# Scans with block loads on ScalarE's queue, later statistics and split stores at the turns

## The chip, the cores and the metric

The kernel runs on one core of a Trainium2 chip. The metric is the device time of one execution in microseconds (us), the median of the runs shown. Five engines of the core appear below: TensorE (PE, with its weight loads as PEld), VectorE (DVE), ScalarE (ACT), GpSimd (POOL) and SyncE (SP). DMAs are issued by SP, by ScalarE and by GpSimd; each of these engines issues in the order of its own instructions, and a DMA that has to wait holds what stands behind it on that engine.

## The reference

The input `x` has the shape (4, 48, 256, 256), float32. Four layers follow one another, each as `x = x + layer(groupnorm(x))`. Layers 0 and 3 are convolution blocks with an 8 by 8 FFT filter; the change doesn't touch them. Layers 1 and 2 are chains of scans, and they are the concern here:

```python
def step(w, b):
    def f(carry, inp):
        nxt = inp + _conv1d(carry, w, b)   # 5 taps, 48 to 48 channels, along the line
        return (nxt, nxt)
    return f
# down: over the rows h = 0 .. 255        up: back over the rows, same weights
# right: over the columns w = 0 .. 255    left: back over the columns
```

Every step needs the line before it, so a scan is a chain of 255 small convolutions. The layer's output is the result of the left scan added to `x`. The group norm of the next layer needs mean and variance of that sum, so they are gathered in the left scan.

## The kernel before

**Pairs.** The four images are two pairs (`NP` = 2), each with 2 x 48 = 96 partitions. The partition's halves hold, by the stage, two images or two interleaved halves of a line. The two pairs are independent chains, and the kernel alternates between them line by line, so that TensorE works for one while VectorE finishes the line of the other.

**A line.** `conv` (L488) issues three matmuls into a PSUM tile `acc`; VectorE then adds bias and the incoming line, which gives the next `line` (L547 down, L587 up, L630 right, L668 left). TensorE's next convolution of that pair needs it. The order of TensorE and VectorE is the order of the program text; SP, ScalarE and GpSimd are ordered by a scheduler.

**Strips and blocks.** A scan goes in strips of `RB` = 8 lines, so 32 strips. The lines of a strip lie in one of three rotating line buffers per pair. What a strip takes in is loaded into the pool `in1` (three buffers per pair) by SP: L525 (down, from `x`), L575 (up), L616 (right, from `up`), L651 (left, from `rt`). Four strips, `BK` = 32 lines, make a block. The tile `blk` of a block comes from the pool `blk1`, which has three buffers, shared by the two pairs.

**Up scan.** At the end of a strip ScalarE copies the lines, turned, into `blk` (L592, two copies per pair). At the end of a block GpSimd stores `blk` to the DRAM tensor `up` (L601). For the last block (`h0 == 0`) each store is cut in two: the part that the first strips of the right scan read (`lo`, 8 columns) and the rest (`hi`).

**Right scan.** It reads strips of `up`. The first two strips load the blocks that were stored earlier first, and the last block apart (L616). Its lines go to the DRAM tensor `rt` (L636).

**Left scan.** At the start of a block SP loads the block's part of `x` into `blk` (L656, two DMAs of 1536 KB per pair). After each strip GpSimd adds the lines onto `blk` (L676, two additions per pair: even and odd lines, `f` = 0 and 1; in the last strip VectorE does it). At the end of a block GpSimd stores `blk` to the next `x` (L690, two DMAs of 1536 KB per pair; the last block in sixteen parts). The statistics of a strip, eight `bn_stats` of 0.68 us (L681), are put on a list, `todo`, and VectorE takes one from it after each row of lines of the next strip:

```python
                    if todo:
                        todo.pop(0)()
```

**The next scan.** After layer 1's left scan the down scan of layer 2 loads strips of the new `x` (L525, two DMAs per pair and strip). After layer 2's left scan layer 3 starts with its weights (L722) and its own strips (L787).

Of the kernel before, what the change touches and what calls it, by code (L numbers as in the profile page):

```python
# [11 lines left out]
ALU = mybir.AluOpType  # L12
# [6 lines left out]
BK = 32  # L19
PW = 16  # L20
BH = BK // 2
RB = 8
# [6 lines left out]
class Net:  # L29
# [466 lines left out]
    def scan_layer(self, n, x, xout, scs, stats):  # L496
        nc, W, H, HB, WB, NP = self.nc, self.W, self.H, self.HB, self.WB, self.NP
        pairs, M, RH = range(NP), W // 2, RB // 2
        with self.tc.manual_schedule(engines={mybir.EngineType.PE, mybir.EngineType.DVE}):
# [19 lines left out]
            for h0 in range(0, H, RB):  # L519
                xin, (ln, _, _) = [], next_lines()  # L520
                for p in pairs:

                    t = own(self.pin, p, [CC, 2, 2, WB, RH, BH], "in")
                    for f in range(2):
                        nc.sync.dma_start(  # L525
                            half(t, f).rearrange("p i e v h w -> p (i e v) (h w)"),
                            x[p, :, :, :, :, f, h0 // 2 : h0 // 2 + RH, :].rearrange(
                                "c i e v h w -> c (i e v) (h w)"
                            ),
                        )  # L530
# [31 lines left out]
            for h0 in range(H - RB, -1, -RB):  # L562
# [26 lines left out]
                for p in pairs:  # L589
                    k = h0 % BK  # L590
                    for e in range(2):
                        nc.scalar.copy(  # L592
                            blk[p][:, :, e, :, k // 2 : k // 2 + RH],
                            inner(ln[p][:, e::2]).rearrange("p h i w -> p i w h"),
                        )
                if h0 % BK == 0:

                    for lo, hi in ((0, RB), (RB, M)) if h0 == 0 else ((0, M),):
                        for p in pairs:
                            for f in range(2):  # L600
                                nc.gpsimd.dma_start(  # L601
                                    self.up[p, :, :, :, h0 // BK, f, lo:hi].rearrange("c i e w h -> c (i e) (w h)"),
                                    half(blk[p], f)[:, :, :, lo:hi].rearrange("p i e w h -> p (i e) (w h)"),
                                )
# [37 lines left out]
            todo = []  # L642
            coming("down", "right")
            for w0 in range(W - RB, -1, -RB):
                (ln, last, _), new = next_lines(), []
                for p in pairs:
# [6 lines left out]
                    if (w0 + RB) % BK == 0:  # L653
                        blk[p] = own(self.pblk, 0, [CC, 2, 2, M, BH], "blk")
                        for e in range(2):
                            nc.sync.dma_start(  # L656
                                half(blk[p], e).rearrange("p i f h w -> p i (f h w)"),
                                x[p, :, :, e, w0 // BK].rearrange("c i f h w -> c i (f h w)"),
                            )
                for r in range(RB - 1, -1, -1):  # L660
# [9 lines left out]
                    if todo:  # L670
                        todo.pop(0)()
                for p in pairs:
                    k = w0 % BK
                    for f in range(2):
                        part = blk[p][:, :, f, :, k // 2 : k // 2 + RH]
                        (nc.vector if w0 == 0 else nc.gpsimd).tensor_tensor(  # L676
# [18 lines left out]
            for f in todo:  # L695
                f()
# [434 lines left out]
```

## Time and profile before

| | |
|---|---|
| median of three runs | 14960.64 us (14956.08 to 14967.43) |
| the profiled execution | 14980.35 us, its span 14978.6 us |
| granted TensorE clock, mean | 0.977 |
| TensorE matmul busy | 13946.2 us (93%) |
| VectorE busy | 4877.0 us (33%) |
| ScalarE busy | 3020.6 us (20%) |
| GpSimd busy | 1441.9 us (10%) |

By the start times of their lines the scans of layer 1 run from 3544 (down), 4209 (up), 4904 (right) and 5567 (left) to 6479 us, those of layer 2 from 6521 to 9454 us. Everything before and after is layers 0 and 3.

A row of the groups of instructions reads: line, engine, operation, output<-input, shapes, count | busy time in us, mean ns of one | idle time of the engine just before them, and what ended most of it. A row of the table of waits reads: who waited <- for whom: us in total, times, the longest. A row of the timeline reads: start, length, engine, line, operation, tiles, count, and in brackets the idle time before it with what ended it. Times of a profile are those of one execution.

### The profile page before, as it was taken

What the parts mean: (1) busy time and instruction counts of PE and PEld (TensorE: products, weight loads), DVE (VectorE), ACT (ScalarE), POOL (GpSimd) and SP (SyncE); (2) the same over time, 40 slices, a digit from 0 to 9 for tenths busy, and PEclk for the clock granted to TensorE, in tenths of its full rate; (3) what the DMA queues carried; (4) which work ended last, traced back from release to release, by engine and by line L of the source; (5) the groups of instructions that cost most, each with busy time, mean ns of one, the idle gap of its engine ahead of it and who ended that gap; (6) DMA issues with size and microseconds to landing.
All of it is one profiled execution on the core that took longest, in us unless ns stands there. A gap on an engine that the chain in (4) does not pass through costs nothing.

```text
span 14978.6 us, 417023 instructions
## 1 busy us (share of the span) xinstructions
PE 13946.2 (93%) x194676; PEld 8914.0 (60%) x194676; DVE 4877.0 (33%) x11205; ACT 3020.6 (20%) x2908; POOL 1441.9 (10%) x1249
## 2 busy tenths in 40 slices
PE   2999999998999997789999977799999999999999
PEld 1444444446777675567777755465656666666666
DVE  5333333333333334433333344222222222222222
ACT  1222222222223000012330000122222222222222
POOL 0000000000000014310000144100000000000000
PEclk9999999999999998899999988899999999999999
DMA  7122222215755877677557767211111110111110
GB/s 160 47 53 47 49 51 49 51 42 102 152 140 142 162 154 158 152 146 153 136 152 156 153 154 164 48 24 19 24 19 20 23 22 17 24 20 23 19 24 18
DMA packets 1165501, 1224.06 MB, mean 82 GB/s; under 512 B 1024900, under 2 KB 1026428, under 8 KB 1102908
## 3 DMA queue, kind: packets, MB, share of 16 engines
q1 hardware_dynamic: 1075388, 750.26, 26.3%
q0 software_dynamic: 88384, 447.12, 10.9%
q8 instruction: 1527, 25.02, 0.7%
q14 instruction: 202, 1.65, 0.0%
HBM read 699.82 MB, written 497.42 MB: 80 GB/s over the span
## 4 chain that ended last, share of the span: by engine, by line
PE 83%; issue 6%; DMA 5%; POOL 4%; DVE 2%; SPq 1%; ACT 0%; DVEq 0%; POOLq 0%; ACTq 0%
PE acc L493 27%; PE pd L882 19%; PE pd L270 13%; PE pp L865 8%; PE pz L834 4%; PE ph L245 3%; DMA blk<-x 3%; POOL blk L676 3%; PE po L910 2%; PE pf L823 2%; PE po L355 2%; PE pf L333 1%; PE py L302 1%; DMA gx<-in_x 1%; PE pt L809 1%
## 5 line engine op out<-in xcount | busy, mean ns | idle before, releaser
L493 PE MATMUL acc<-line,w_down 96*96 96x256 f32 x12240 | 2650.2, 379 | 42.8 <-ACT line L534 24.9
L493 PEld LDWEIGHTS acc<-line,w_down 96*96 96x96 f32 x12240 | 1995.8, 163 | 696.6 <-issue 42.9
L493 PE MATMUL acc<-line,w_left 96*96 96x256 f32 x6120 | 1371.2, 386 | 452.4 <-DVE line L668 452.2
L270 PE MATMUL pd<-main,diag 32*32 32x512 f32 x36864 | 1671.2, 599 | 32.4 <-issue 32.3
L882 PE MATMUL pd<-z_a,diag 32*32 32x512 f32 x37152 | 1673.8, 597 | 5.8 <-DVE g_m L897 5.3
L882 PE MATMUL pd<-z_b,diag 32*32 32x512 f32 x37152 | 1651.7, 596 | 14.4 <-DVE g_a L897 13.4
L493 PEld LDWEIGHTS acc<-line,w_left 96*96 96x96 f32 x6120 | 1013.0, 166 | 810.3 <-DVE line L668 476.4
L493 PE MATMUL acc<-line,w_right 96*96 96x256 f32 x6120 | 1330.0, 380 | 65.5 <-DVE line L627 40.1
L865 PEld LDWEIGHTS pp<-c_idft,z 128*128 128x128 f32 x10240 | 1156.9, 181 | 288.7 <-issue 187.0
L865 PE MATMUL pp<-c_idft,z 128*128 128x128 f32 x10240 | 1224.1, 278 | 19.3 <-ACT z_b L869 18.7
L493 PEld LDWEIGHTS acc<-line,w_right 96*96 96x96 f32 x6120 | 1000.2, 164 | 395.3 <-DVE line L627 42.1
L836 DVE TENSOR_TENSOR z<-pz,mask 128x512 f32<-128x512 f32 x1024 | 701.4, 685 | 1431.2 <-PE pz L834 1431.2
L270 PEld LDWEIGHTS pd<-main,diag 32*32 32x32 f32 x36864 | 594.1, 103 | 656.2 <-issue 534.7
L270 PE MATMUL pd<-rest,diag 32*32 32x512 f32 x18432 | 938.1, 597 | 24.6 <-issue 24.6
L882 PEld LDWEIGHTS pd<-z_a,diag 32*32 32x32 f32 x37152 | 638.5, 103 | 491.6 <-issue 306.0
L882 PEld LDWEIGHTS pd<-z_b,diag 32*32 32x32 f32 x37152 | 593.2, 103 | 490.5 <-issue 304.3
L676 POOL TENSOR_TENSOR blk<-blk,line 96x1024 f32<-96x1024 f32 x248 | 703.9, 2865 | 1075.8 <-DVE line L668 575.2
L630 DVE SCALAR_TENSOR_TENSOR line<-acc,b_right,in 96x256 f32<-96x256 f32 x1020 | 489.4, 480 | 836.2 <-PE acc L493 836.2
L587 DVE SCALAR_TENSOR_TENSOR line<-acc,b_down,in 96x256 f32<-96x256 f32 x992 | 476.0, 480 | 808.6 <-PE acc L493 808.6
L547 DVE TENSOR_TENSOR line<-acc,in 96x256 f32<-96x256 f32 x1020 | 429.3, 421 | 928.0 <-PE acc L493 928.0
L102 ACT ACTIVATE nrm<-nrm 96x2 f32<-96x2 f32 (+1 forms) x4 | 0.8, 204 | 3512.2 <-DVE nrm L101 3512.2
L592 ACT COPY blk<-line 96x1024 f32<-96x1024 f32 x256 | 481.3, 1943 | 934.7 <-DVE line L587 741.4
(138 smaller groups left out, 12063.2 us busy)
## 6 DMA issues: line engine op xcount, KB each, us to landing
in<-x SPq DMA_DIRECT2D x256, 384.0 KB, 10.6
blk<-x SPq DMA_DIRECT2D x64, 1536.0 KB, 28.4
dn<-line POOLq DMA_DIRECT2D x124, 768.0 KB, 9.5
rt<-line POOLq DMA_DIRECT2D x124, 768.0 KB, 10.2
in<-rt SPq DMA_DIRECT2D x124, 768.0 KB, 7.4
in<-dn SPq DMA_DIRECT2D x120, 768.0 KB, 8.0
in<-up SPq DMA_DIRECT2D x240, 384.0 KB, 11.1
up<-blk POOLq DMA_DIRECT2D x56, 1536.0 KB, 23.9
```

Of the source, the lines that this page charges most:

```text
L245: nc.tensor.matmul(ph[to, b, 0 : r1 - r0, :], wi[s, at : at + m], xn[s, r0:r1, :], start=True, stop=True)
L270: nc.tensor.matmul(pd[32 * j : 32 * j + 32, i], diag[s, img // 2, t, :], z[s, R2 * j + t // 3 : R2 * j + t // 3 + R2, t % 3 : t % 3 + W], ...
L493: self.nc.tensor.matmul(acc, w[:, t, :], carry[:, :, t : t + m], start=(t == 0), stop=(t == 2))
L547: nc.vector.tensor_tensor(blocks(inner(line)), blocks(acc), xin[p][:, :, r % 2, :, r // 2, :], ALU.add)
L587: nc.vector.scalar_tensor_tensor(inner(line), acc, bd, new[p][r], ALU.add, ALU.add)
L592: nc.scalar.copy(blk[p][:, :, e, :, k // 2 : k // 2 + RH], inner(ln[p][:, e::2]).rearrange("p h i w -> p i w h"),)
L630: nc.vector.scalar_tensor_tensor(blocks(inner(line)), blocks(acc), br, new, ALU.add, ALU.add)
L676: (nc.vector if w0 == 0 else nc.gpsimd).tensor_tensor(part, part, inner(ln[p][:, f::2]).rearrange("p w i h -> p i h w"), ALU.add)
L834: nc.tensor.matmul(pz[:, b, 0 : 2 * HD], xf[s, q, :], wi[s, :], start=True, stop=True)
L836: nc.vector.tensor_tensor(z[:, q, 0 : 2 * n].rearrange("p (b c) -> p b c", b=2), pz[:, :, 0:n], mask[:, :, 0:n].to_broadcast([128, 2, n]), ...
L865: nc.tensor.matmul(pp[0:n, q // 4, :, q % 4 * PW : (q % 4 + 1) * PW], z[:, q0 + q, k * NM : k * NM + n], self.idft, start=True, stop=True,)
L882: nc.tensor.matmul(pd[32 * j : 32 * j + 32, i, 0:n, :], diag[s, 2 if g == "m" else half, t, :], zt[g][s, R2 * j + t // 3 : R2 * j + t // 3 ...
```

## The change

Four edits, all in `scan_layer`:

1. *Down scan, first strip.* The load of the strip is cut: per half `f`, `i` and `e` one DMA for the blocks 1 to 7 and then one for block 0, 16 DMAs per pair instead of 2. Other strips are loaded as before.
2. *Up scan.* ScalarE's copies into `blk` and the stores of `blk` are in one loop over the parts. In the last strip every copy is cut into `lo` and `hi`, and the `lo` parts are stored by ScalarE's queue; all else is stored by GpSimd.
3. *Left scan, loads and statistics.* The loads of `blk` are issued on ScalarE's queue. The eight statistics of a strip are taken one after each line (of either pair) in the last four rows of the next strip, not one after each row from its first.
4. *Left scan, additions and stores.* They are in one loop by parts and pairs, so that a pair's stores follow its additions. In the last strip VectorE's additions are cut into `lo` and `hi`, `lo` of both pairs first, and ScalarE's queue stores the `lo` parts.

```diff
                     for f in range(2):
-                        nc.sync.dma_start(
-                            half(t, f).rearrange("p i e v h w -> p (i e v) (h w)"),
-                            x[p, :, :, :, :, f, h0 // 2 : h0 // 2 + RH, :].rearrange(
-                                "c i e v h w -> c (i e v) (h w)"
-                            ),
-                        )
+                        rows = x[p, :, :, :, :, f, h0 // 2 : h0 // 2 + RH, :]
+                        if h0:
+                            nc.sync.dma_start(
+                                half(t, f).rearrange("p i e v h w -> p (i e v) (h w)"),
+                                rows.rearrange("c i e v h w -> c (i e v) (h w)"),
+                            )
+                            continue
+
+                        for lo, hi in ((1, WB), (0, 1)):
+                            for i in range(2):
+                                for e in range(2):
+                                    nc.sync.dma_start(
+                                        half(t, f)[:, i, e, lo:hi].rearrange("p v h w -> p v (h w)"),
+                                        rows[:, i, e, lo:hi].rearrange("c v h w -> c v (h w)"),
+                                    )
...
-                for p in pairs:
-                    k = h0 % BK
-                    for e in range(2):
-                        nc.scalar.copy(
-                            blk[p][:, :, e, :, k // 2 : k // 2 + RH],
-                            inner(ln[p][:, e::2]).rearrange("p h i w -> p i w h"),
-                        )
-                if h0 % BK == 0:
-
-                    for lo, hi in ((0, RB), (RB, M)) if h0 == 0 else ((0, M),):
-                        for p in pairs:
-                            for f in range(2):
-                                nc.gpsimd.dma_start(
-                                    self.up[p, :, :, :, h0 // BK, f, lo:hi].rearrange("c i e w h -> c (i e) (w h)"),
-                                    half(blk[p], f)[:, :, :, lo:hi].rearrange("p i e w h -> p (i e) (w h)"),
-                                )
+
+                for lo, hi in ((0, RB), (RB, M)) if h0 == 0 else ((0, M),):
+                    for p in pairs:
+                        k = h0 % BK
+                        for e in range(2):
+                            nc.scalar.copy(
+                                blk[p][:, :, e, lo:hi, k // 2 : k // 2 + RH],
+                                inner(ln[p][:, e::2])[..., lo:hi].rearrange("p h i w -> p i w h"),
+                            )
+                        for f in range(2) if h0 % BK == 0 else ():
+                            (nc.scalar if hi < M else nc.gpsimd).dma_start(
+                                self.up[p, :, :, :, h0 // BK, f, lo:hi].rearrange("c i e w h -> c (i e) (w h)"),
+                                half(blk[p], f)[:, :, :, lo:hi].rearrange("p i e w h -> p (i e) (w h)"),
+                            )
...
                         for e in range(2):
-                            nc.sync.dma_start(
+                            nc.scalar.dma_start(
                                 half(blk[p], e).rearrange("p i f h w -> p i (f h w)"),
                                 x[p, :, :, e, w0 // BK].rearrange("c i f h w -> c i (f h w)"),
                             )
+                ripe, fresh = fresh, []
                 for r in range(RB - 1, -1, -1):
                     for p in pairs:
...
-                    if todo:
-                        todo.pop(0)()
+                        if ripe and r < RB // 2:
+                            ripe.pop(0)()
+                k = w0 % BK
+
+                for lo, hi in ((0, RB), (RB, M)) if w0 == 0 else ((0, M),):
+                    for p in pairs:
+                        for f in range(2):
+                            part = blk[p][:, :, f, lo:hi, k // 2 : k // 2 + RH]
+                            (nc.vector if w0 == 0 else nc.gpsimd).tensor_tensor(
+                                part, part, inner(ln[p][:, f::2])[..., lo:hi].rearrange("p w i h -> p i h w"), ALU.add
+                            )
+                        for e in range(2) if k == 0 else ():
+                            for f in ((0, 1), (1, 2)) if w0 == 0 else ((0, 2),):
+                                f = slice(*f)
+                                (nc.scalar if hi < M else nc.gpsimd).dma_start(
+                                    xout[p, :, :, e, w0 // BK, f, lo:hi].rearrange("c i f h w -> c i (f h w)"),
+                                    half(blk[p], e)[:, :, f, lo:hi].rearrange("p i f h w -> p i (f h w)"),
+                                )
                 for p in pairs:
...
+                            to, t = stats[2 * p + i][:, w0 // RB * 2 + f, :], blk[p][:, i, f, :, k // 2 : k // 2 + RH]
+                            fresh.append(lambda to=to, t=t: nc.vector.bn_stats(to, t))
```

The number of bytes moved and the arithmetic are the same.

## The prediction

> **What bounds the kernel now.** I read the slices first: TensorE is busy nearly everywhere except in slices 16 to 18 and 24 to 26, the two left scans. Then the costliest groups, for the same convolution in the right and the left scan:
>
> ```profile
> L493 PE MATMUL acc<-line,w_left 96*96 96x256 f32 x6120 | 1371.2, 386 | 452.4 <-DVE line L668 452.2
> ...
> L493 PE MATMUL acc<-line,w_right 96*96 96x256 f32 x6120 | 1330.0, 380 | 65.5 <-DVE line L627 40.1
> ...
> L676 POOL TENSOR_TENSOR blk<-blk,line 96x1024 f32<-96x1024 f32 x248 | 703.9, 2865 | 1075.8 <-DVE line L668 575.2
> ```
>
> Both scans have 6120 matmuls of nearly one duration, but TensorE idles 452.4 us ahead of those of the left scans and 65.5 us ahead of those of the right. All of it waits for VectorE's line update, L668, so next the table of waits for what holds VectorE:
>
> ```profile
> DVE st L681 <- POOL blk L676: 507.3, 61, 32.4
> POOL blk L676 <- DMA blk<-x: 500.5, 14, 38.0
> ```
>
> VectorE waits 507.3 us at L681, the statistics, for GpSimd's addition; GpSimd waits 14 times, 500.5 us, for the block load. The statistics stand between line updates, so TensorE stops behind them. The timeline shows both waits; I call 5647.48, where the last strip of a block starts its additions, T0.
>
> ```profile
> 5647.48 8.52 POOL L676 TENSOR_TENSOR blk<-blk,line 96x1024 f32<-96x1024 f32 x3 [10.84 <-DVE line L668]
> ...
> 5656.04 0.69 DVE L681 BATCH_NORM_STATS2 st<-blk 96x6 f32<-96x512 f32 x1 [2.16 <-POOL blk L676]
> 5656.30 0.54 POOL L690 DMA_DIRECT2D x<-blk  x1 [0.29 <-POOL blk L676]
> ...
> 5659.66 1.67 POOL L690 DMA_DIRECT2D x<-blk  x3
> ...
> 5676.72 16.97 SPq L656 DMA_DIRECT2D blk<-x  x4
> ...
> 5715.48 5.63 POOL L676 TENSOR_TENSOR blk<-blk,line 96x1024 f32<-96x1024 f32 x2 [37.54 <-DMA blk<-x]
> 5718.33 0.69 DVE L681 BATCH_NORM_STATS2 st<-blk 96x6 f32<-96x512 f32 x1 [31.92 <-POOL blk L676]
> ...
> 5719.46 34.18 PE L493 MATMUL acc<-line,w_left 96*96 96x256 f32 x144 [30.98 <-DVE line L668]
> ```
>
> In every strip the first statistic waits for three additions (8.52 us) and comes 2.16 us late. A strip then repeats every 22.17 us; the right scan needs 20.72 (the chain of waits, from 7943.30 to 8523.48, 28 strips), so 1.45 us is lost. At a block's end the wait is 31.92 us: pair 1's new block reuses the buffer of pair 0's old one (three buffers, four blocks wanted), so its load goes out only when pair 0's second store has landed (5659.66 plus its 16.9 us) and lands at 5715.48, T0+68. After such a stop the clock is low (columns of the windows: length, busy time and instructions of PE, PEld, DVE, ACT, POOL, then granted clock, DMA share, GB/s):
>
> ```profile
> 5720.00:5725.00 5.00, 5.00 (x13) 3.39 (x12) 0.94 (x3) 0.00 (x0) 3.17 (x2) 0.50 0.71 177
> 5725.00:5730.00 5.00, 5.00 (x24) 3.70 (x23) 3.06 (x6) 0.00 (x0) 5.00 (x3) 0.97 0.54 128
> ```
>
> 13 matmuls in 5 us instead of 24: 144 matmuls take 34.18 us against 31.32 before the stop, 2.9 us more. The seven stops of a scan repeat every 118.2 us; 4 strips of 20.72 are 82.9, so **35.3 us is lost per block**, and a left scan takes 912 us, some 250 over 664.
>
> The turns from up to right cost about 35 us each:
>
> ```profile
> 4871.06 1.13 POOL L601 DMA_DIRECT2D up<-blk  x2 [2.11 <-ACT blk L592]
> 4872.88 3.38 POOL L601 DMA_DIRECT2D up<-blk  x6 [0.69 <-ACT blk L592]
> 4873.77 30.18 SPq L616 DMA_DIRECT2D in<-up  x16
> 4893.85 0.29 DVE L627 COPY line<-in 96x256 f32<-96x256 f32 x1 [24.83 <-DMA in<-up]
> ...
> 4903.70 0.29 DVE L627 COPY line<-in 96x256 f32<-96x256 f32 x1 [9.56 <-DMA in<-up]
> ```
>
> The 16 small loads (24 KB, packets of 256 B) need 30 us on SP while four stores of 1440 KB drain; pair 1 is complete only when the stores are.
>
> **What the Trainium skill says.** "DMA: Bandwidth & Descriptors", section "Issuing engines are not separate DMA queues": another issuing engine saves only its sequencer's time; the transfers share the same engines. So moving the block loads gives no bandwidth; the trace agrees, the DMA share being about 1.0 all through T0+10 to T0+68. The same page, "Queues, rings and completion order": each DMA engine takes turns between queue rows, a packet at a time. The turn agrees: from 4880 to 4888, 222 packets of the hardware queue and 279 of the software queue moved, nearly one for one, but 0.05 MB against 1.97. "TensorE: Matmul & The Clock Gate", "What's actually happening": the clock halves after some 3.4 us of idling; the window above shows it.
>
> **The change part by part.**
>
> *Statistics later.* Same 8 per strip, 0.68 us each, now one after each line of the last four rows. The first is due 11.7 us after the strip's start instead of 2.6; the third addition is done some 4.7 us after it. All ordinary waits go: 1.45 us × 3 per block. Cover on VectorE: a line is due every 1.295 us, update and statistic are 0.48 + 0.68 = 1.16; in the slots that hold a statistic now VectorE still idles 0.22 us for TensorE, so I cost them at nothing. Without that cover 0.1 us a slot would be 51 us (512 slots).
>
> *Block loads on ScalarE's queue.* ScalarE computes nothing in a left scan, so a waiting load blocks nothing there, and on SP the loads of `rt` no longer stand behind it (they end no wait now: nothing). The load still waits for pair 0's store. In the changed kernel's order GpSimd does pair 0's f=1, pair 1's f=1, pair 0's f=0, then both stores of pair 0 (T0+8.8 and T0+9.4, before +8.8 and +12.2), pair 1's f=0, and then **the first addition of the next strip before pair 1's stores**: these leave at T0+23.7 instead of +12.7. Pair 0's two stores follow one another in one queue (12.0 us for the first, 8.3 more for the second), so both land at T0+27 to 29. Then 3.15 MB of pair 1's load, nearly all of 3.15 MB of pair 1's stores and about 1.2 MB of `rt` are in flight, 7 MB. Before, 8.6 MB moved from T0+29.2 to T0+68 (with a part of the following block's load, which is now out later): 221 GB/s. 7 MB take 32 us: **landing at T0+60** (55 if stores and load overlap at the 250 to 280 GB/s of the windows with mixed traffic; 65 if they go one after the other).
>
> *What the stop becomes.* Pair 1's first statistic is due at T0 + 2 × 20.72 = T0+41.4 (it was T0+38.9) and needs one addition after the landing: 60 + 2.85 − 41.4 = 21 us, plus 2.9 for the clock: 24 instead of 35.3. The following strip's additions are queued behind and catch up: they end 11.4 us after the late pair, half a strip before their statistics. Per scan 7 × 11.3 + 4 (first block) = 83 us, **two scans 166 us gained** (96 to 236 for landings at T0+65 and T0+55).
>
> *Up to right.* ScalarE's copies are split, but in the changed order narrow and wide slices alternate, and pair 1's narrow store leaves after all four pairs of copies, at 4875.2 instead of about 4873. No gain there. SP has one load of the next strip ahead of pair 1's four, and ScalarE's queue sends pair 1's first block (3.15 MB) as soon as pair 0's wide store lands, about 4888 (wide stores took 11.7 to 19.4 us), into the drain. Block transfers move in packets of some 14 KB (448 for 6.29 MB); with 16 KB that is 12 for each of 16 DMA engines, each about 1 us at a sixteenth of 250 GB/s and one turn that SP's small packets wait: 12 us, and 3 for the extra load. So 15 us later, two turns: **30 us lost**. Bounds: 5 us won in all, if the smaller queue on GpSimd drains earlier, to 50 lost, if the second block's load joins too.
>
> *First strip of the down scans.* 16 loads per pair instead of 2. Layer 1: all issue after the norm at 3532; 32 × 0.5 us puts pair 1's last issue at 3548, its landing near 3553 against 3545.4 now, so it loses 8 (3 to 14). Layer 2: seven eighths are loaded ahead; only 16 of 12 KB remain, behind the small stores that now leave on ScalarE at about 6481. They suffer from the wide stores as at the other turn, 48 packets per DMA engine at 0.57 us: ready about 6513 against 6521: 7 won (0 to 16; the norm, ready at 6502, is the next thing late). Layer 3: its weights wait for the last store; GpSimd issues 8 instead of 16, and no longer waits for queue slots (1.57 us): 5 won (0 to 6). Sum +4.
>
> **Sum:** 166 − 30 + 4 = 140 us. Against the profiled execution (14980.35, of it 1.75 outside the span) this is 14840; the runs shown have a median 20 us lower, 14960.64, so I forecast **14820**.
>
> **Rivals.**
> *A, likeliest (0.60):* as above; its own range, with the bounds added, 14730 to 14910.
> *B, the load lands no earlier (0.15):* two stores and a load finish together as late as before (T0+66.5 on average). Stop 27.5 + 2.9; gain 2 × (7 × 4.9 + 4) = 77, minus 26: 14910. For it: the DMA engines were full already. Against it: the other block's load leaves the interval.
> *C, slower (0.13):* the delayed stores of pair 1 starve the load at the block's end. If the stores drain first (some 4.3 MB with `rt` from T0+28, at 200 GB/s until T0+50) and the load then needs 28 us, the median landing of a block load on the page, it lands at T0+78: stop 39 + 2.9, 6.6 more than before; 2 × (7 × 6.6 − 4) = 84 lost, and 26 at the turns: 15070. It decides from a landing at about T0+70 on. For it: the stores leave 11 us later, right ahead of the load. Against it: the one-for-one turns seen above.
> *D, the stop nearly goes (0.12):* pair 0's stores, alone in their queue, land at T0+22 and the load at T0+48: stop 9 + 2.9; gain 2 × (7 × 23.4 + 4) − 26 = 310: 14650. Against it: the first store alone took 12 us.
>
> **How the numbers follow.** 0.2% is 30 us, about what a measurement of this kernel can tell from no change. A is faster in nearly all of its range, B mostly, D wholly: 0.81. Same 0.07, from the edges of A and B. Slower 0.12, C. The range of 14680 to 14930 holds A, B and the near edge of D; it leaves out C and most of D.
>
> **What would show it.** Right: the first statistic of a strip waits for nothing in three strips of four; strips of 20.7 us; seven stops per left scan of 16 to 26 us behind the DMA of `blk`; left scans near 830 us; 40 to 55 us at the up-to-right turns; layer 1's start 8 us later. Wrong: stops over 31 us (C) or under 12 (D); TensorE idle behind the packed statistics in the last four rows; a right scan whose loads are late in its third strip.

## The result and the profile after

The changed kernel takes **14795.3 us** (median of 4 runs, 14786.4 to 14797.92) against 14964.03 us before: a ratio of 0.9886, 95% interval 0.9869 to 0.9903, or 169 us less. The forecast was 14820 us. The profiled execution has a span of 14796.1 us and a mean granted clock of 0.981 (before 0.977).

The costliest groups first: the same convolution in the left and in the right scan, and GpSimd's additions.

```profile
L493 PE MATMUL acc<-line,w_left 96*96 96x256 f32 x6120 | 1359.4, 385 | 252.0 <-DVE line L676 252.0
L493 PE MATMUL acc<-line,w_right 96*96 96x256 f32 x6120 | 1338.9, 381 | 103.4 <-DVE line L637 38.9
...
L686 POOL TENSOR_TENSOR blk<-blk,line 96x1024 f32<-96x1024 f32 x248 | 705.8, 2874 | 864.8 <-DVE line L676 445.8
```

TensorE's idle time in the left scans fell from 452.4 to 252.0 us. In the right scans it rose from 65.5 to 103.4. GpSimd's additions are as many as before and as long (2874 ns against 2865). The table of waits says which waits shrank:

```profile
POOL blk L686 <- DMA blk<-x: 419.0, 14, 32.6
...
DVE st L700 <- POOL blk L686: 275.9, 28, 21.6
```

VectorE's wait at the statistics fell from 507.3 us (61 times) to 275.9 (28 times, two at each of 14 stops): the waits of ordinary strips are gone, those at a block's end are shorter. The timeline at the first block's end (T0 = 5656.41, where GpSimd starts the additions of the block's last strip):

```profile
5651.07 0.68 DVE L700 BATCH_NORM_STATS2 st<-blk 96x6 f32<-96x512 f32 x1
5651.96 0.48 DVE L676 SCALAR_TENSOR_TENSOR line<-acc,b_left,in 96x256 f32<-96x256 f32 x1 [0.21 <-PE acc L493]
...
5656.41 8.52 POOL L686 TENSOR_TENSOR blk<-blk,line 96x1024 f32<-96x1024 f32 x3 [9.37 <-DVE line L676]
...
5665.23 1.09 POOL L692 DMA_DIRECT2D x<-blk  x2 [0.29 <-POOL blk L686]
...
5679.93 1.10 POOL L692 DMA_DIRECT2D x<-blk  x2
...
5682.56 27.60 ACTq L663 DMA_DIRECT2D blk<-x  x4
...
5714.24 16.96 POOL L686 TENSOR_TENSOR blk<-blk,line 96x1024 f32<-96x1024 f32 x6 [30.31 <-DMA blk<-x]
5717.10 0.69 DVE L700 BATCH_NORM_STATS2 st<-blk 96x6 f32<-96x512 f32 x1 [19.33 <-POOL blk L686]
...
5718.23 11.95 PE L493 MATMUL acc<-line,w_left 96*96 96x256 f32 x46 [18.39 <-DVE line L676]
```

The first two rows are an ordinary slot: a statistic, then the line update, which still waits 0.21 us for TensorE, so the statistic is hidden. Then both stores of pair 0 leave at T0+8.8, those of pair 1 at T0+23.5; pair 1's new block is asked for at T0+26.2, GpSimd adds at T0+57.8, and TensorE has stood still for 18.4 us.

The turn from up to right, layer 1:

```profile
4859.40 1.26 ACTq L608 DMA_DIRECT2D up<-blk  x2
...
4862.34 31.45 SPq L623 DMA_DIRECT2D in<-up  x16
...
4888.61 0.29 DVE L634 COPY line<-in 96x256 f32<-96x256 f32 x1 [29.57 <-DMA in<-up]
...
4893.27 0.29 DVE L634 COPY line<-in 96x256 f32<-96x256 f32 x1 [4.36 <-DMA in<-up]
...
4895.52 25.89 ACTq L663 DMA_DIRECT2D blk<-x  x4
...
4947.65 0.48 DVE L637 SCALAR_TENSOR_TENSOR line<-acc,b_right,in 96x256 f32<-96x256 f32 x1 [12.95 <-DMA in<-up]
...
4958.35 0.87 DVE L637 SCALAR_TENSOR_TENSOR line<-acc,b_right,in 96x256 f32<-96x256 f32 x2 [10.23 <-DMA in<-up]
```

The two pairs start at 4888.61 and 4893.27 (in the kernel before at 4893.85 and 4903.70, its up scan ending 10 us later). But ScalarE sends four block loads, 6.3 MB (pair 1's first block and pair 0's second), from 4895.52 on, and the third strip's lines come late: the updates at 4947.65 and 4958.35 end waits of 12.95 and 10.23 us for the load of `in`.

Taken from the start times of VectorE's line updates, first to last line of a scan, layers 1 and 2 (us). A landing is read as the end of GpSimd's wait for the block:

| | before | after |
|---|---|---|
| left scans | 911.1, 909.5 | 805.3, 803.2 |
| right scans | 662.2, 662.4 | 686.0, 686.4 |
| last line of up to first convolved line of right | 35.4, 35.5 | 34.9, 35.0 |
| last line of layer 1's left scan to first line of layer 2 | 42.8 | 38.9 |
| landing of pair 1's block, mean of 14 | T0+66.2 | T0+57.4 |

The profiled spans differ by 182.5 us, 13 more than the medians. That much lies in layer 0, which ends 13.4 us earlier in this execution (scale of the norm, L110, at 3507.5 against 3520.9); two kernels with the same layer 0, told of below, have it at 3509.9 and 3519.3. It is scatter between executions.

### The profile page after: what moved, and what is told of

The parts are those of the page before. It is cut to its first block, busy times and chain, and to the rows that moved or that the text cites. A ratio compares the mean times of both kernels' runs of the same rounds, so it can differ in the third digit from the quotient of the medians.

```text
span 14796.1 us, 417160 instructions
## 1 busy us (share of the span) xinstructions
PE 13940.6 (94%) x194676; PEld 8922.0 (60%) x194676; DVE 4880.6 (33%) x11213; ACT 3022.1 (20%) x2916; POOL 1429.3 (10%) x1225
## 4 chain that ended last, share of the span: by engine, by line
PE 89%; DMA 6%; DVE 1%; SPq 1%; issue 1%; POOL 1%; ACT 0%; ACTq 0%; DVEq 0%; POOLq 0%
PE acc L493 32%; PE pd L889 19%; PE pd L270 13%; PE pp L872 8%; PE pz L841 4%; PE ph L245 3%; DMA blk<-x 3%; PE po L917 2%; PE pf L830 2%; PE po L355 2%; PE pf L333 1%; PE py L302 1%; DMA x<-blk 1%; DMA gx<-in_x 1%; POOL blk L686 1%
## 5 line engine op out<-in xcount | busy, mean ns | idle before, releaser
L889 PE MATMUL pd<-z_b,diag 32*32 32x512 f32 x37152 | 1651.0, 596 | 14.0 <-DVE g_a L904 13.1
L493 PE MATMUL acc<-line,w_left 96*96 96x256 f32 x6120 | 1359.4, 385 | 252.0 <-DVE line L676 252.0
L493 PE MATMUL acc<-line,w_right 96*96 96x256 f32 x6120 | 1338.9, 381 | 103.4 <-DVE line L637 38.9
L686 POOL TENSOR_TENSOR blk<-blk,line 96x1024 f32<-96x1024 f32 x248 | 705.8, 2874 | 864.8 <-DVE line L676 445.8
L603 ACT COPY blk<-line 96x1024 f32<-96x1024 f32 (+2 forms) x264 | 482.0, 1889 | 935.7 <-DVE line L596 755.9
## 6 DMA issues: line engine op xcount, KB each, us to landing
blk<-x ACTq DMA_DIRECT2D x64, 1536.0 KB, 23.3
up<-blk POOLq DMA_DIRECT2D x56, 1536.0 KB, 23.8
```

Source lines behind the costliest of these rows:

```text
L493: self.nc.tensor.matmul(acc, w[:, t, :], carry[:, :, t : t + m], start=(t == 0), stop=(t == 2))
L603: nc.scalar.copy(blk[p][:, :, e, lo:hi, k // 2 : k // 2 + RH], inner(ln[p][:, e::2])[..., lo:hi].rearrange("p h i w -> p i w h"),)
L686: (nc.vector if w0 == 0 else nc.gpsimd).tensor_tensor(part, part, inner(ln[p][:, f::2])[..., lo:hi].rearrange("p w i h -> p i h w"), ALU.add)
L889: nc.tensor.matmul(pd[32 * j : 32 * j + 32, i, 0:n, :], diag[s, 2 if g == "m" else half, t, :], zt[g][s, R2 * j + t // 3 : R2 * j + t // 3 ...
```

## The experiments

Two questions stood after the comparison. Which of the three edits of the left scan moved the landing from T0+66 to T0+57? And what made the second stop of the right scans? My theory was that the order of the stores did the first and ScalarE's queue the second. The lengths of scans are again those of the profiled execution, layers 1 and 2. The kernel before was measured again beside each group of runs: its median was 14971.28 us beside the first four experiments (the three single edits and the one with all block loads back on SP), 14970.72 and 14967.41 beside the later ones. In two of the expectations 893 and 787 stand for a second left scan; they are layer 1's scan counted without its first strip (18 us), so 912 and 805 are the figures to compare with.

### Single edits on the kernel before

*Statistics alone.*

```diff
-                    if todo:
-                        todo.pop(0)()
+                        if ripe and r < RB // 2:
+                            ripe.pop(0)()
```

> The kernel before with one edit: the eight statistics of a strip are taken in the last four rows of the next strip, as in the changed kernel. Loads, stores and turns are those of before. Theory: the edit takes away the 1.45 us of each ordinary strip (two per block remain in the table of before besides the stop, four in the first block) and puts the deadline of pair 1's first statistic from T0+38.9 to T0+41.4. The block load still lands at T0+66 (mean of the 14 stops before: 66.3), so a stop is 66.3 + 2.9 - 41.4 = 28 us and a block repeats every 113 us: 5.4 won per block, 14 blocks and the two first blocks: about 87 us faster than before, near 14877. Rival (the transfers set the period): the strips get shorter, the load lands later by the same amount, and under 30 us are won. Rival (VectorE has no room in the last four rows): TensorE loses 0.1 us or more in 512 slots, and the gain shrinks to 35 us.

Measured: 14876.3 us, ratio 0.9938 (0.9923 to 0.9952). Left scans 863.4 and 867.0 us, 90 less in the sum against 87 expected; landing unchanged at T0+66.1. VectorE's waits for the additions:

```profile
DVE st L682 <- POOL blk L677: 397.5, 28, 29.7
```

28 waits instead of 61: only those at a block's end are left. The price of the statistics and the later deadline was right, and neither rival holds.

*Queue alone.*

```diff
-                            nc.sync.dma_start(
+                            nc.scalar.dma_start(
                                 half(blk[p], e).rearrange("p i f h w -> p i (f h w)"),
```

> The kernel before with one edit: the block loads of the left scans are issued on ScalarE's queue instead of SP's. Theory (the order of the stores, not the queue, makes the load land earlier): landing stays at T0+65 to T0+68, the left scans stay within 10 us of 912 and 893, and the right scans get the second stop of the changed kernel (some 23 us in the third strip), because ScalarE sends the first blocks' loads into the turn: 40 to 50 us slower than before, near 15010. Rival (the queue of its own makes the load land earlier): landing at T0+57 to T0+60, 8 us won in each of 14 blocks, 112 us, less the 47 us at the turns: 14900. Rival (the second stop comes from the changed order of the small stores and loads at the turn, not from the block loads): no second stop here, and no change.

Measured: 14982.85 us, ratio 1.0009 (1.0000 to 1.0017): no gain. It is two effects that cancel. The left scans take 889.5 and 895.0 us, 36 less in the sum (landing T0+63.6, a third of the way, which I had not expected), and the right scans 685.6 and 686.1 us, 47 more, with the same stop in the third strip. So the second stop belongs to the queue: here no store at the turn was changed. The 36 us are the landing, 2.6 us in each of 14 stops.

*Stores pair by pair alone.*

```diff
                 for p in pairs:
...
+                    if k == 0 and w0:
+                        for e in range(2):
+                            nc.gpsimd.dma_start(
+                                xout[p, :, :, e, w0 // BK].rearrange("c i f h w -> c i (f h w)"),
+                                half(blk[p], e).rearrange("p i f h w -> p i (f h w)"),
+                            )
...
```

> The kernel before with one edit: in the left scan a pair's two stores follow that pair's additions, so that pair 0's go out at T0+8.8 and T0+9.4; pair 1's still go out at about T0+12.5, ahead of the next strip's additions. Loads on SP, statistics and turns as before. Theory: pair 0's second store lands 3 us earlier, the load goes out at T0+26 and lands at T0+62 to T0+64 (the stores of pair 1 are not late, so the mixture of transfers is that of before): 3 to 4 us won per block, 14 blocks, 40 to 55 us faster, near 14915. Rival (the order of the stores alone makes the whole difference): landing at T0+57.5, 8.8 us per block, 123 us faster. Rival (it is the queue or the delayed stores of pair 1): landing at T0+66, no change.

Measured: 14866.04 us, ratio 0.9933 (0.9918 to 0.9948). Left scans 861.4 and 860.5 us, 99 less in the sum, twice what my theory gave. The load left no earlier, at T0+29.7, but landed at T0+59.1. The order of the stores matters, then, but not by way of an earlier start of the load. SP's queue at the first block's end (T0 = 5631.24):

```profile
5633.78 1.60 SPq L651 DMA_DIRECT2D in<-rt  x2
5660.95 2.57 SPq L656 DMA_DIRECT2D blk<-x  x2
5663.62 3.64 SPq L651 DMA_DIRECT2D in<-rt  x2
5680.02 0.55 SPq L656 DMA_DIRECT2D blk<-x  x1
```

SP issues in order: the loads of `rt` follow 0.10 us after the end of the block loads that had waited ahead of them (5660.95 + 2.57 = 5663.52). In the kernel before (T0 = 5647.48) two loads of `rt` left at T0+2.5 and T0+3.8, as here, but the next two at T0+24.7 and T0+26.0, and only then, from 5676.72 on, four of `blk`. Here two loads of `rt` (one strip, 1.57 MB) stand behind pair 1's block instead of ahead of it, and only one of pair 0's next two block loads follows within 20 us, not both. SP's order is the scheduler's work, and the edit of the stores had moved it. Whether this reordering makes the earlier landing is not shown by this run; it is taken up below.

### Putting edits together and taking one away

*The changed kernel with all block loads back on SP.* The diff is that of the queue, reversed.

> The changed kernel with one edit undone: all block loads of the left scans are issued on SP again. Theory (the order of the stores makes the load land early, the queue makes the second stop of the right scans): landing stays at T0+57 to T0+60, the left scans stay within 10 us of 805 and 787 us, and the stop of 23.5 us in the third strip of both right scans goes: 45 us faster than the changed kernel, near 14750. Rival (the queue makes the landing early): landing back at T0+66, 8.8 us per block lost, 123 us, and 47 won at the turns: 14870. Rival (loads of the lines standing behind a waiting block load on SP): a strip's lines from rt come late, with stops at other strips than the block's end.

Measured: 14756.68 us, ratio to before 0.9856 (0.9840 to 0.9872), 39 us under the changed kernel (46, if each is set against the kernel before that was measured beside it). Left scans 803.1 and 804.3, landing T0+57.2; right scans 662.5 and 661.5, no second stop. My theory held: beside the other two edits the queue brings nothing in the left scans and costs 47 us at the turns.

*The kernel before with statistics and stores edited, no edit at the turns.*

> The kernel before with two edits: statistics in the last four rows and stores pair by pair. No edit at the turns, loads on SP. With both edits the order on GpSimd has the next strip's first addition ahead of pair 1's stores, as in the changed kernel (with the stores alone it had not). Theory: left scans of 803 us as in the changed kernel with its loads on SP, and everything else as before: the edits at the turns are worth no more than 8 us together, so 14757 to 14770, 205 us faster than before. Rival (the two edits only add up: 90 and 99 us in the left scans): 14780. Rival (the small stores on ScalarE's queue and the split first strips carry more than that): 14775 or above, or below 14745 if they cost.

Measured: 14751.6 us, ratio 0.9853 (0.9839 to 0.9868). Left scans 803.1 and 802.7 us, landing T0+57.3. The two edits are worth 215 us together where they gave 90 and 99 alone: with both, pair 1's stores leave at T0+23.5 instead of T0+13.1, the load leaves at T0+25.8 instead of T0+29.7, and it lands 1.8 us earlier than with the stores alone, 25 us in 14 blocks. The edits at the turns are worth nothing that these medians show (14756.68 with them, 14751.6 without).

*Pair 1's stores early, on ScalarE's queue.*

```diff
-                                (nc.scalar if hi < M else nc.gpsimd).dma_start(
+                                (nc.scalar if hi < M or (p and w0) else nc.gpsimd).dma_start(
```

> The changed kernel with the block loads on SP, and pair 1's stores of all blocks but the last on ScalarE's queue, so that no addition of the next strip stands ahead of them: they leave at T0+12 to T0+13 instead of T0+23.5. Theory (the late stores help pair 0's stores to land early and hardly hurt the load): pair 1's load leaves at T0+29 instead of T0+26 and lands at T0+59 instead of T0+57.2; 2 us more in each of 14 stops, 14785. Rival (the late stores starve the load, as my third case had it): landing at T0+50 or earlier, 7 us less in each stop, 14660. Rival (on a queue of their own the stores of the two pairs share evenly, so pair 0's land with pair 1's at T0+30 and both loads go out together as before): landing at T0+64 to T0+66, 7 to 9 us more in each stop, 14870.

Measured: 14745.88 us, ratio 0.9850 (0.9835 to 0.9864). None of the three cases. The load left at T0+33, 7 us later than with the late stores, and still landed at T0+57.0. So the moment of issue isn't what sets the landing. The late stores of pair 1 do not starve the load, and sending them early wins nothing at the landing.

*The first block's loads on SP, later ones on ScalarE's queue.*

```diff
+                        queue = nc.sync if w0 + RB > W - BK else nc.scalar
                         for e in range(2):
-                            nc.scalar.dma_start(
+                            queue.dma_start(
...
```

> The changed kernel with the first block's loads of each left scan (both pairs) on SP, all later ones on ScalarE's queue. At the turn from up to right ScalarE then sends only pair 0's second block, 3.15 MB, instead of 6.3 MB, while the third strip's loads (1.57 MB in packets of 256 B) are on their way. Theory (the second stop is the third strip waiting for block traffic, so it goes by bytes): 3.15 MB less at some 200 GB/s are 16 us less, the stop in the third strip falls from 23.5 to about 8 us (0 to 12), and the kernel stands 30 us under the changed kernel, at 14765. Rival (what counts is that a block load goes out at all while the small packets wait for their turns): the stop stays at 20 us or more. Rival (it was the first block alone, sent earliest): the stop is gone, 14755.

Measured: 14738.55 us (two runs), ratio 0.9846 (0.9826 to 0.9866). Right scans 662.3 and 661.5 us: the stop is gone altogether. The trace takes the ground from under the comparison of 3.15 with 6.3 MB:

```profile
4895.62 0.54 SPq L664 DMA_DIRECT2D blk<-x  x1
...
5485.28 22.58 ACTq L664 DMA_DIRECT2D blk<-x  x2
```

ScalarE's first block load left at 5485 us, near the end of the right scan, and none of ScalarE's fell into the turn. Why pair 0's second block waited so long I don't know. What follows is only that it is enough to keep the first block off ScalarE's queue. Nor does every block load at the turn make a stop: here SP itself sent 1.57 MB of pair 0's first block at 4895.62, ahead of the third strip's loads, and in the kernel before it sent 3.15 MB at 4907.32, both without one. Whether the stop comes from the amount (6.3 MB) or from the second queue beside SP's was not separated.

### What sets the landing

*Pair 0's later blocks not loaded.*

```diff
-                        for e in range(2):
+                        for f in range(4) if p == 0 and w0 + RB < W else ():
+                            to = blk[p][:, f // 2, f % 2].rearrange("p h w -> p (h w)")
+                            nc.scalar.copy(to, bl[:, 0:1].to_broadcast([CC, M * BH]))
+                        for e in range(2) if p or w0 + RB == W else ():
```

> The kernel before with one thing taken out: from the second block on, pair 0's blocks are not loaded from x; the idle ScalarE fills them from the bias with four copies of 96x2048 instead, so pair 0's part of the sum is left out. Order of stores, queues, statistics and pair 1's loads are those of before. In the kernel before, pair 1's load leaves at T0+29 and shares the DMA engines from T0+45 on with pair 0's following block (3.15 MB). Theory (this competing load, not the moment of issue, makes pair 1's load late; storing pair by pair works because it sends the competitor out later and in halves): pair 1's load still leaves at T0+29 and lands at T0+56 to T0+59 instead of T0+66, the stops are 9 us shorter, 14 of them: about 14840. Rival (the delay comes from stores and from the small loads of lines): landing at T0+64 to T0+66, within 30 us of before.

Measured: 14928.08 us, ratio 0.9970 (0.9959 to 0.9982). Landing T0+63.4: the competing load costs 2.8 us, not 9. My theory fell. Another took its place: pair 1's block lands when the bytes that SP and GpSimd have queued ahead of it and beside it have moved. The DMA view, from T0+5 to the landing (63.5 us), of the kernel before at a block of layer 2 (q1 is SP's queue):

```profile
DMA packets 1165, 13.60 MB, mean 214 GB/s; under 512 B 165, under 2 KB 165, under 8 KB 165
...
q1 hardware_dynamic: 716, 7.29, 59.3%
```

The same stretch (53.6 us) with stores pair by pair:

```profile
DMA packets 983, 11.70 MB, mean 218 GB/s; under 512 B 139, under 2 KB 139, under 8 KB 139
...
q1 hardware_dynamic: 533, 5.37, 52.1%
```

And in the changed kernel (53.1 us), where q10 is ScalarE's queue:

```profile
DMA packets 1122, 12.96 MB, mean 244 GB/s; under 512 B 160, under 2 KB 160, under 8 KB 160
...
q1 hardware_dynamic: 406, 2.80, 20.3%
...
q10 hardware_dynamic: 267, 3.85, 31.5%
```

The software queue (q0, GpSimd's stores) moves 6.29 MB in each. With stores pair by pair 1.9 MB fewer pass ahead of the landing, at nearly the same rate (218 against 214 GB/s): 1.9 MB at 215 GB/s are 8.8 us for a landing that comes 9.9 us earlier at these two blocks. The kernel with pair 1's stores early moved 11.77 MB at 226 GB/s, though its load left 7 us later. At nearly one rate fewer bytes up to a landing and an earlier landing are almost one statement. Which bytes matter can only be seen by taking some out. Pair 0's following load, taken out above, is a first answer: over the 14 stops 12.22 MB moved at 209 GB/s instead of 13.36 at 218, so 1.14 MB less won 2.8 us, about half of what they take at the old rate (1.14 MB at 218 GB/s are 5.2 us). Why the rate fell isn't known.

*The last strip of a block not loaded from `rt`,* the two loads that stood ahead:

```diff
-                        nc.sync.dma_start(t.rearrange("p r i h -> p r (i h)"), self.rt[p, :, w0 : w0 + RB, :])
+                        if w0 % BK == 0:
+                            nc.scalar.copy(t.rearrange("p r i h -> p (r i h)"), bl[:, 0:1].to_broadcast([CC, RB * W]))
+                        else:
+                            nc.sync.dma_start(t.rearrange("p r i h -> p r (i h)"), self.rt[p, :, w0 : w0 + RB, :])
```

> The kernel before, with the last strip of each block of the left scan not loaded from rt: ScalarE fills its tile from the bias (96x2048, about 2 us a copy), so those lines are left out. In the kernel before these two loads, 1.57 MB, go out on SP at about T0+23 to T0+28 just ahead of pair 1's block load. Theory (pair 1's load lands when the bytes ahead of it and beside it have moved, at 210 to 220 GB/s; 13.6 MB are moved from T0+5 to its landing, storing pair by pair puts one strip's lines behind the block load and so lands at T0+59): without these bytes the load lands at T0+59 to T0+60 instead of T0+66.2, every stop is 6.5 us shorter, 14 stops: 90 us faster than before, near 14880. Rival (the moment at which pair 0's stores land is all that counts): landing at T0+64 to T0+66.

*The second strip not loaded,* as many bytes, at another place (`w0 % BK == 2 * RB`):

> The kernel before, with the second strip of each block not loaded from rt but filled by ScalarE in the same way: as many bytes are left out as with the last strip, but they would have moved ahead of T0, when the DMA engines are a third busy. Theory (only the bytes between T0 and the landing count): landing stays at T0+65 to T0+67, and the kernel is within 30 us of before. Rival (the bytes of a whole block set its period): as much is won as with the last strip left out, about 90 us.

Measured: without the last strip 14848.87 us (two runs), ratio 0.9920 (0.9900 to 0.9939), landing T0+57.6, somewhat earlier than expected; without the second 14967.84 us, ratio 1.0001 (0.9992 to 1.0011), landing T0+66.5. The DMA view of one block each, from T0+5 to the landing, first without the last strip, then without the second:

```profile
DMA packets 908, 11.57 MB, mean 222 GB/s; under 512 B 128, under 2 KB 128, under 8 KB 128
...
DMA packets 1159, 13.53 MB, mean 215 GB/s; under 512 B 165, under 2 KB 165, under 8 KB 165
```

The same bytes are worth 118 us in one place and nothing in the other, so what counts is whether they stand between T0 and the landing. Over the 14 stops the run without the last strip moved 1.83 MB less than the kernel before, at the same rate (219 and 218 GB/s): 8.4 us, for a landing that comes 8.6 us earlier. In these two runs, then, bytes ahead of the block load cost their full time, and those of the later load beside it about half.

### A faster version

The stop is the way of one buffer from pair 0's store to pair 1's load. Half a buffer goes round sooner:

```diff
-                        blk[p] = own(self.pblk, 0, [CC, 2, 2, M, BH], "blk")
+                        blk[p] = [own(self.pblk, 0, [CC, 2, M, BH], "blk") for _ in range(2)]
...
+                        for f in range(2):
+                            for e in range(2):
+                                nc.sync.dma_start(
+                                    half(blk[p][f], e).rearrange("p i h w -> p i (h w)"),
+                                    x[p, :, :, e, w0 // BK, f].rearrange("c i h w -> c i (h w)"),
+                                )
```

> The changed kernel with the block loads on SP, and each block in two tiles, one for even and one for odd lines (six buffers of 16 KB per partition instead of three of 32), each loaded, added to, stored and released by itself. Theory (the stop is the way of one buffer from pair 0's store to pair 1's load, so half a buffer goes round faster): pair 0's first half is stored at T0+6 to T0+9, lands at about T0+18, its statistics are taken by T0+17 to T0+20, so 1.57 MB of pair 1 can leave near T0+20 and land at T0+42 to T0+48; the first addition needs no more. Stop 4 to 9 us, and 2 for the clock: 11 to 14 us won in each of 14 blocks, 14580 (14550 to 14620). Rival (the DMA engines are the bound: 18.9 MB per block at 200 GB/s are 94 us, 11 us over four strips): 14630 whatever the buffers do. Rival (packets of 8 KB instead of 16 KB and twice the issues eat it): within 30 us of 14757.

Measured: **14588.4 us**, ratio to before 0.9746 (0.9729 to 0.9762), 207 us under the changed kernel. Left scans 751.3 and 734.6 us. The groups:

```profile
L493 PE MATMUL acc<-line,w_left 96*96 96x256 f32 x6120 | 1382.5, 389 | 106.3 <-DVE line L678 106.3
L493 PE MATMUL acc<-line,w_right 96*96 96x256 f32 x6120 | 1329.3, 379 | 32.6 <-DVE line L635 20.4
```

The timeline at one block's end (T0 = 5716.28), the load of the first half and the two halves of the stop:

```profile
5736.30 9.31 SPq L665 DMA_DIRECT2D blk<-x  x4
...
5756.75 2.86 POOL L688 TENSOR_TENSOR blk<-blk,line 96x1024 f32<-96x1024 f32 x1 [11.48 <-DMA blk<-x]
...
5759.64 0.69 DVE L700 BATCH_NORM_STATS2 st<-blk 96x6 f32<-96x512 f32 x1 [2.00 <-POOL blk L688]
...
5766.74 14.08 POOL L688 TENSOR_TENSOR blk<-blk,line 96x1024 f32<-96x1024 f32 x5 [7.14 <-DMA blk<-x]
5769.60 0.69 DVE L700 BATCH_NORM_STATS2 st<-blk 96x6 f32<-96x512 f32 x1 [7.90 <-POOL blk L688]
```

The first half leaves at T0+20.0 and is added at T0+40.5, the second at T0+50.5; the stop is two waits of 2.00 and 7.90 us. The load leaves just as the last of pair 0's four statistics ends (5736.23), and by the table of waits SP waits 4.4 us for the statistics ahead of a block load in this stretch, so these may be what is late next; that wasn't tried. The turns, too, took 19.0 us instead of 35, which I had not expected: ScalarE waits on its queue (3.41 us for a store, 4.68 with nothing shown), its last wide copies (those for the `hi` parts) come after that, and so six of the eight wide stores leave at 4864.6 to 4868.0 us, when eight of the sixteen small loads have been issued (4852.95 to 4864.23).

*With the wide stores put last,* on SP behind the first strip's loads:

> The kernel with half tiles, and the wide parts of the last block of the up scan stored on SP behind the first strip's loads of the right scan (one of the eight stays ahead of them). With half tiles the turn took 19 us instead of 35, because ScalarE's queue held the wide copies back, so that part of the small loads passed ahead of the wide stores. Theory (small loads are slow only while wide stores are in flight): the first line of the right scan comes 12 to 15 us after the last of the up scan; but the second strip's last parts wait for the wide stores, which now land some 30 us after the turn, so that a stop of 5 to 15 us appears in the second strip, and the sum is within 10 us of 14588. Rival (the wide stores drain faster undisturbed and the second strip comes in time): 10 us less at each turn, 14568. Rival (stores on SP hold up the loads behind them): a stop of over 20 us, 14610 or more.

Measured: 14604.34 us, ratio 0.9759 (0.9742 to 0.9775), slower by 16 us than without it, where I expected at most 10 either way. The right scan starts 12.6 us after the up scan, and a stop in its second strip takes that back, as the theory had it (the two right scans are 13 and 16 us longer): from the last line of up to the end of the right scan 687.8 and 690.8 us, against 680.9 and 681.1 with half tiles alone. That is the whole difference.

## Why the prediction was right, point by point

| step | predicted | measured |
|---|---|---|
| left scans, both | −166 | −212 |
| turns up to right | +30 | +47 |
| layer 1's start | +8 | +3.5 |
| layer 2's start | −7 | −3.9 |
| layer 3's start | −5 | about −2 |
| sum | −140 | −167 |
| medians | −140 (14820) | −169 |

The sum came closer than its terms: the left scans won 46 us more and the turns lost 17 us more than I had reckoned, and that these two errors partly cancel is luck.

**Ordinary strips** went as predicted, and the packed statistics cost nothing: the slot still shows 0.21 us of idle time.

**The stop** was the mis-sized term. Its chain was right: stores at T0+8.8 and +23.5, load issued at about T0+26 (I had T0+27 to 29), deadline T0+41.4. The landing was T0+57.4, not 60, and the low clock after the shorter stop cost 1.8 us, not 2.9 (in the first 5 us after it the granted clock was 0.64, before 0.50): 57.4 + 2.9 − 41.4 + 1.8 = 20.7 us per block instead of 24. That is 3.3 us in 14 blocks, the missing 46 us. I took 7 MB after the stores' landing at 221 GB/s, the rate of the kernel before. The trace has 12.96 MB at 244 GB/s over the whole stretch. Over all 14 stretches of a kernel the mean is 244 in the changed kernel and 245 in the one that differs from it only in the first block's queue. It is 223 with all block loads on SP, and 223 with ScalarE's queue alone. So the queue brings the higher rate, but only beside the other two edits; why is open. I had reckoned with no gain in bandwidth from it.

**What I credited was partly wrong.** I had the queue as harmless in the left scan and the late stores of pair 1 as a risk. The runs show that the late stores decide nothing at the landing, and that the queue takes the place of an effect that I had not seen at all: with the new order of stores SP would have put one strip's lines behind the block load. With ScalarE's queue those lines move beside it (2.80 MB on q1 before the landing), and at the higher rate the load lands at the same time (T0+57.4 against 57.2 on SP).

**The turns** have the right cause in the wrong place. I let ScalarE's block loads collide with pair 1's small loads in the first strip. But they left at 4895.5, not 4888, when both first strips were in; the first stop is 0.5 us shorter than before. They met the third strip's loads instead, which the prediction named as a sign against it, and the second block's load did join, which was its worst case (50 lost): 23.8 and 24.0 us per right scan instead of 15.

**The starts** are within their bounds. Layer 1: first line 24.7 us after the scale of the norm instead of 23.3, and 2.1 us more behind it. Layer 3: from the last line of the left scan to the end 5522.0 us, in eight kernels with the old order 5522.3 to 5525.7.

**The rivals.** B and D are out by their landings (T0+66.5, T0+48). C (T0+78) is out by its landing too, and its cause by the run with pair 1's stores early: T0+57.0 against 57.2. B's stop has a slip: its own figures, 66.5 + 2.85 − 41.4, give 28.0 us, not 27.5, some 6 us in 14 blocks.

## What to carry to other kernels

When DMA engines are full, count the bytes that stand ahead of the transfer that ends the wait, queue by queue, and not the moment of its issue: taking 1.57 MB out of the right place won 118 us, out of another place nothing. The rate has to be measured too: here it was 209 to 245 GB/s, by the mixture. A load that moves to an idle engine's queue also moves in time, since nothing there holds it back (pair 1's first block left at 4895.5 us instead of 5513.1): look where it lands in the stage before. Where two edits come together, run each alone: here one of three, the queue, brought all of the loss at the turns and, beside the other two, none of the gain.

## What the runs showed that I had not expected

An edit of one queue reordered another: storing pair by pair changed which loads of lines the scheduler put ahead of the block load on SP, and by the run without the last strip's loads a large part of its 99 us comes from there. With the DMA engines full from T0+5 to the landing and stores and loads of 16 and 8 KB rows mixed, the means of 14 stretches were 209 to 225 GB/s in ten kernels with whole tiles; only the changed kernel and the one with its first block's loads on SP reached 244 and 245. The Trainium skill, "DMA: Bandwidth & Descriptors", section "Latency and other measured facts", gives 207 GB/s for copies between tensors in memory whose rows per partition lie 512 KiB apart. In a pair's part of `x` a channel of two images takes 2 x 256 x 256 x 4 bytes, 512 KiB. The lower rates are alike, but the changed kernel reached 244 with the same distance, so it can't be the whole cause; no run changed it.
